# A recurrent kernel on one core: half A of the state chunk by chunk, and the x side of eight steps as seven block products

## The chip, the cores and the metric

The kernel runs on one core of a Trainium2 chip. The metric is the time of one execution on the device in microseconds; the kernel before takes 1693.7 us (median of three runs, 1693.68 to 1693.88). The engines are PE (matmul, with PEld for its weight loads), DVE (vector), ACT (scalar), POOL (GpSimd) and SP (which issues the DMAs).

## The reference, cut to what matters

A gated recurrence over 512 steps, for 8 sequences, with 512 inputs and 512 state units, all in float32. The output is x plus the states.

```python
def step(h, x_t):
    fused = sigmoid(concatenate([x_t, h], -1) @ w_W + w_b)
    hidden_state, output_state = split(fused, 2, -1)          # r and z
    memory_state = x_t @ wx_W + wx_b + hidden_state * (h @ wh_W + wh_b)
    h_new = output_state * h + (1.0 - output_state) * tanh(memory_state)
    return h_new, h_new
_, hs = lax.scan(step, h0, swapaxes(x, 0, 1))
return x + swapaxes(hs, 0, 1)
```

So every step needs three products of the state (for r, for z, and h @ wh_W), which wait for the step before, and three products of x, which wait for nothing and can be made for several steps at once.

## The kernel before, in words

**Layout.** State units are laid out in four chunks (`k` = 0 to 3) of 128 partitions. Chunks 0 and 1 are half A, chunks 2 and 3 half B (`hf` = 0, 1). A matmul takes 32 rows (8 sequences of a group of four steps, of which each step uses its own) as the stationary operand and writes 32 partitions of PSUM: the output units are cut into four column blocks (`j` = 0 to 3), each on its own 32 columns of the PE array, `mm(reg[32*j:32*j+32], lhsT, weights[k, j])`. Float32 makes two PE instructions of one matmul.

**The state's products.** Per step, 48 matmuls of 128 columns: banks R (r), G and H (halves of z and of h @ wh_W), each with four chunks and four blocks, in the order of line 27, `R0 R1 G0 G1 R2 R3 G2 G3 H0 H1 H2 H3`. Those with 0 and 1 need half A of the new state, those with 2 and 3 half B. The banks are doubled by groups of four steps, and PSUM accumulates onto what was copied there.

**The x side.** For a group of four steps, `prefill` (line 215) makes 16 matmuls of 384 columns (64 for half of z, 128 for r, 128 for the memory's x part, 64 for the other half of z: columns 64 to 448 of the bank `xp`) into one of two PSUM banks `xps[g % 2]`, in four rows of four blocks. `x_side` strings the groups together, and each step takes one row (line 276), behind the products of the state. `seed` (line 211) puts the biases into the bank before (a copy of 512 columns on ACT), `spread` (227) copies 128 columns each to R, G and H of the group (ACT), and `turn_x` (232) transposes X, the memory's part, to the tile `md1` (DVE).

**The step on DVE and ACT.** `turn_r` transposes r's products (tr) and puts their sigmoid into `md0`; `turn_h` transposes h @ wh_W to `md1`; `turn_z` transposes z's (tz) and puts sigmoid(-z) into `hd0`. `memory` makes r * hh + xx for pairs of slots as one running scan (multiply, add) into m, and its tanh into a slot of the state's tile `hT`; `update` makes the new state as a scan over three slots. They stand in the order tr A, tr B, then h, z, memory and update for half A, then the same for half B. In `scans` (line 280) half A is one scan of both chunks, half B two scans of one chunk; the tiles of half A are laid out rows first, those of half B chunks first (`pair`, line 134).

**Order.** It is written by hand (`manual_schedule`): each engine executes in the order in which the loop issues. At the end of a step stand: copies of the state (ACT), `turn_x` for the next group (DVE), one `spread` or, in the fourth step, `seed` (ACT), three small memsets (DVE), and the output sums x + h on POOL (`add`). The `tr` of half B waits for POOL's sums of seven steps before (line 312), as the tiles of the state go round in eight. SP's queue has the loads of x, three chunks of 16 steps ahead, and the stores of the output.

Of the kernel before, what the change touches and what calls it, by code (L numbers as in the profile page):

```python
# [28 lines left out]
FIRST = "Q0 x Q1 x Q2 x Q3 H0 H1 H2 H3"  # L29

BANKS = ("R", "G", "H")

XP = {"G": slice(0, 128), "R": slice(128, 256), "X": slice(256, 384), "H": slice(384, 512)}

# [2 lines left out]
def tile_cond_rnn_residual(  # L37
# [95 lines left out]

    def pair(n, name, rows, slots):

        if n == "A":
            return const.tile([P, rows, 2, slots], F32, name=name)
        return const.tile([P, 2, rows, slots], F32, name=name).rearrange("p c n s -> p n c s")


# [20 lines left out]
    for t_ in hd0[0] + hd0[1]:  # L161
        nc.gpsimd.memset(t_[:, :, :, 1], -1.0)
    idle = const.tile([P, IDLE], F32, name="idle")

    def state(hf, i, slot=2):

# [10 lines left out]
    def mm(out_, lhsT, rhs, start=False):  # L177
        nc.tensor.matmul(  # L178
            out_, lhsT, rhs, start=start, stop=False, skip_group_check=True
        )  # L180
# [30 lines left out]
    def seed(g):  # L211

        nc.scalar.copy(xps[g % 2], bias)

    def prefill(g):

        c, t0 = divmod(g * GS, TC)
        for k in range(NQ):
            for j in range(NQ):
                mm(  # L220
                    xps[g % 2][32 * j : 32 * j + 32, 64:448],
                    x_of(c, k, t0, GS),
                    wx[:, k, j, :],
                )
            yield

    def spread(g, names):

        for n in names:
            nc.scalar.copy(banks[g % 2][n], xps[g % 2][:, XP[n]])  # L230

    def turn_x(g, e):

        c0 = XP["X"].start + 32 * e
        nc.vector.transpose(
            md1[e // 2][g % 2][:, :, e % 2, 1], xps[g % 2][:, c0 : c0 + 32]
        )

    def take(it, n=None):
# [12 lines left out]
    later = x_side()  # L252
    spread(0, "RGH")
    for e in range(NQ):
        turn_x(0, e)

    pool_done = {}
    for i in range(T):
        g, s = divmod(i, GS)
        c, t = divmod(i, TC)  # L260
        ps = banks[g % 2]
        if t == 0 and c > 0:
            load_x(c + 3)
        if t == 0:
            ot = out_p.tile([P, TC, NQ, B], F32, tag="ot", name=f"ot_{c}")

        for n in (ORDER if i else FIRST).split():
            if n == "x":
                take(later, 1)
                continue  # L270
            bank, k = n[0], int(n[1])
            hs = hT[k // 2][i % NH][:, :, k % 2, 2]
            for j in range(NQ):
                to = xps[0][:, :256] if bank == "Q" else ps[bank]
                mm(to[32 * j : 32 * j + 32, :], hs, wh(bank, k, j))
        take(later, 1)

        rows = slice(B * s, B * s + B)

        def scans(hf, out_, d0, d1):  # L280

            for c_ in [slice(0, 2)] if hf == 0 else [slice(0, 1), slice(1, 2)]:
                nc.vector.tensor_tensor_scan(  # L283
                    *[t_[:, :, c_].rearrange("p n c s -> p (n c s)") for t_ in (out_, d0, d1)],
                    0.0,
                    ALU.mult,
                    ALU.add,
                )
# [12 lines left out]
        def turned(n, hf):  # L301
            t_ = work.tile([P, 2, 32], F32, tag=f"t{n}{hf}", name=f"t{n}{hf}_{i}")
            inst = nc.vector.transpose(t_.rearrange("p c n -> p (c n)"), raw[n][hf]).ins  # L303
# [15 lines left out]

        def turn_h(hf):  # L320
            nc.vector.transpose(  # L321
                md1[hf][g % 2][:, :, :, 0].rearrange("p n c -> p c n"), raw["h"][hf]
            )
# [12 lines left out]

        def memory(hf):

            m = work.tile([P, B, 2, 2] if hf == 0 else [P, 2, B, 2], F32, tag=f"m{hf}", name=f"m{hf}_{i}")
            if hf == 1:  # L340
                m = m.rearrange("p c n s -> p n c s")
# [25 lines left out]
        turn_h(1)  # L367
        turn_z(1)
        memory(1)
        update(1)  # L370
        for hf in range(2):
            act(("h", hf, (i + 1) % NH), state(hf, i + 1, 0), state(hf, i + 1), AF.Copy)
        if i < 3:
            load_x(i + 1)

        if g + 1 < NG:
# [105 lines left out]
```

## Time and profile before

| | us |
|---|---|
| median of three runs | 1693.7 |
| span of the profiled execution | 1691.7 |
| PE busy | 1680.3 (99%) |
| PE weight loads busy | 1467.6 (87%) |
| DVE busy | 1087.0 (64%) |
| ACT busy | 915.5 (54%) |
| POOL busy | 231.2 (14%) |
| matmuls of the x side, busy | 431.3, 4032 instructions, 486 ns each |

The profiled execution has no time of its own beside the span; the span is set against the median. Matmuls overlap each other (four column blocks, and one behind the other), so the busy time of a group counts more than its share of the step: what a group takes is read from the starts in the timeline. In the timeline a line merges neighbours of one kind; the bracket names the idle time before it and what ended it. PE ran at full granted clock (1.000) for the whole span. Nothing of note moves on the DMA queues after the start (17 GB/s).

### The profile page before, as it was taken

The page shows a single profiled execution, that of the slowest core. Times are in us where ns is not written, and L with a number is a line of the kernel's source. Part 1 is how long each engine was busy: PE and PEld are TensorE (multiplying, and loading weights), DVE is VectorE, ACT ScalarE, POOL GpSimd, SP SyncE. Part 2 cuts the span into 40 slices and gives each one's busy share as a digit, 9 for nine tenths or more (in the row PEclk, how much of TensorE's full clock was granted, in tenths as well). Part 3 has the DMA queues.
Part 4 walks back from the last instruction along what each step waited for, and adds up shares of the span by engine and source line. Part 5 has one row for each costly group of instructions (what it writes and reads, how often), then busy time and mean ns, then how long its engine had stood idle before and what let it go on. Part 6 is the DMA issues. An engine that isn't in the chain of part 4 may idle for free.

```text
span 1691.7 us, 121258 instructions
## 1 busy us (share of the span) xinstructions
PE 1680.3 (99%) x53230; PEld 1467.6 (87%) x53230; DVE 1087.0 (64%) x8229; ACT 915.5 (54%) x5121; POOL 231.2 (14%) x1032
## 2 busy tenths in 40 slices
PE   8999999999999999999999999999999999999998
PEld 6888888888888888888888888888888888888887
DVE  5666666666666666666666666666666666666666
ACT  3555555555555555555555555555555555555554
POOL 0111111111111111111111111111111111111111
PEclk9999999999999999999999999999999999999999
DMA  4000000000000000000000000000000000000000
GB/s 177 17 17 5 17 17 17 17 4 17 17 17 17 4 17 17 17 17 13 9 18 17 17 17 4 17 17 17 17 5 17 17 17 17 4 17 11 11 11 10
DMA packets 11483, 30.86 MB, mean 18 GB/s; under 512 B 1220, under 2 KB 1732, under 8 KB 10952
## 3 DMA queue, kind: packets, MB, share of 16 engines
q1 hardware_dynamic: 10800, 22.94, 3.9%
q8 instruction: 416, 6.82, 1.7%
q14 instruction: 115, 0.94, 0.2%
q10 hardware_dynamic: 152, 0.16, 0.0%
HBM read 14.70 MB, written 8.39 MB: 14 GB/s over the span
## 4 chain that ended last, share of the span: by engine, by line
PE 98%; DMA 1%; DVE 0%; ACT 0%; issue 0%; SPq 0%
PE R L178 26%; PE G L178 26%; PE H L178 26%; PE xp L178 19%; DMA whh<-in_whh_dram 1%; DMA head<-in_xh_dram 0%; DVE md1A L321 0%; DVE hTA L283 0%; ACT hd0A L205 0%; ACT hTA L205 0%; SPq L124 0%; DVE tz L303 0%; ACT hTB L205 0%; DVE hTB L283 0%; ACT hd0B L205 0%
## 5 line engine op out<-in xcount | busy, mean ns | idle before, releaser
L178 PE MATMUL xp<-wx,xin 128*32 128x384 f32 x4032 | 431.3, 486 | 0.0
L178 PEld LDWEIGHTS R<-wgr,hTA 128*32 128x32 f32 x8176 | 247.4, 135 | 206.8 <-DVE hTA L283 206.4
L303 DVE STREAM_TRANSPOSE tr<-R 128x64 f32<-128x64 f32 x1022 | 194.4, 229 | 309.1 <-PE R L178 309.1
L178 PE MATMUL R<-wgr,hTA 128*32 128x128 f32 x8176 | 330.9, 273 | 2.2 <-DVE hTA L283 2.2
L178 PE MATMUL H<-whh,hTA 128*32 128x128 f32 x8192 | 331.3, 273 | 0.8 <-DMA whh<-in_whh_dram 0.8
L178 PE MATMUL H<-whh,hTB 128*32 128x128 f32 x8192 | 331.2, 273 | 0.0
L178 PE MATMUL R<-wgr,hTB 128*32 128x128 f32 x8176 | 330.6, 273 | 0.0
L178 PE MATMUL G<-wgr,hTB 128*32 128x128 f32 x8176 | 330.6, 273 | 0.0
L178 PE MATMUL G<-wgr,hTA 128*32 128x128 f32 x8176 | 330.6, 273 | 0.0
L385 POOL TENSOR_TENSOR ot<-xin,hTB 128x16 f32<-128x16 f32 x503 | 126.4, 251 | 1415.6 <-DVE hTB L283 1324.0
L205 ACT ACTIVATE hd0B<-tz 128x16 f32<-128x16 f32 x512 | 114.9, 224 | 305.3 <-DVE tz L303 305.3
L205 ACT ACTIVATE md0A<-tr 128x16 f32<-128x16 f32 x512 | 119.6, 234 | 265.2 <-DVE tr L303 265.2
L178 PEld LDWEIGHTS H<-whh,hTA 128*32 128x32 f32 x8192 | 260.2, 136 | 1.2 <-DMA whh<-in_whh_dram 1.2
L178 PEld LDWEIGHTS G<-wgr,hTA 128*32 128x32 f32 x8176 | 259.8, 136 | 0.0
L178 PEld LDWEIGHTS H<-whh,hTB 128*32 128x32 f32 x8192 | 254.5, 122 | 0.0
L178 PEld LDWEIGHTS G<-wgr,hTB 128*32 128x32 f32 x8176 | 254.1, 122 | 0.0
L178 PEld LDWEIGHTS R<-wgr,hTB 128*32 128x32 f32 x8176 | 245.2, 122 | 0.0
L283 DVE TENSOR_TENSOR_SCAN hTA<-hd0A,hTA 128x48 f32<-128x48 f32 x512 | 132.1, 258 | 149.2 <-ACT hTA L205 149.2
L283 DVE TENSOR_TENSOR_SCAN hTB<-hd0B,hTB 128x24 f32<-128x24 f32 x1024 | 158.1, 196 | 104.0 <-ACT hTB L205 104.0
L205 ACT ACTIVATE hd0A<-tz 128x16 f32<-128x16 f32 x512 | 118.9, 232 | 111.4 <-DVE tz L303 111.4
L321 DVE STREAM_TRANSPOSE md1A<-G 128x64 f32<-128x64 f32 x511 | 156.8, 307 | 28.7
L205 ACT ACTIVATE hTB<-hTB 128x16 f32<-128x16 f32 x512 | 121.2, 237 | 81.1 <-DVE hTB L283 80.5
(62 smaller groups left out, 1680.2 us busy)
## 6 DMA issues: line engine op xcount, KB each, us to landing
xin<-in_x_dram SPq DMA_DIRECT2D x31, 256.0 KB, 3.8
out_dram<-ot SPq DMA_DIRECT2D x31, 256.0 KB, 3.3
wx<-in_wx_dram SPq DMA_DIRECT2D x4, 768.0 KB, 7.2
wgr<-in_wgr_dram SPq DMA_DIRECT2D x4, 512.0 KB, 9.7
whh<-in_whh_dram SPq DMA_DIRECT2D x1, 768.0 KB
whh<-in_wh_dram SPq DMA_DIRECT2D x1, 256.0 KB, 11.2
out_dram<-ot SPq DMA_DIRECT2D x1, 192.0 KB, 1.9
head<-in_xh_dram ACTq DMA_DIRECT2D x1, 144.0 KB, 5.2
```

The lines of the kernel that those rows point to most:

```text
L178: nc.tensor.matmul(out_, lhsT, rhs, start=start, stop=False, skip_group_check=True)
L205: inst = nc.scalar.activation(out_, in_, func, **kw).ins
L283: nc.vector.tensor_tensor_scan(*[t_[:, :, c_].rearrange("p n c s -> p (n c s)") for t_ in (out_, d0, d1)], 0.0, ALU.mult, ALU.add,)
L303: inst = nc.vector.transpose(t_.rearrange("p c n -> p (c n)"), raw[n][hf]).ins
L321: nc.vector.transpose(md1[hf][g % 2][:, :, :, 0].rearrange("p n c -> p c n"), raw["h"][hf])
L385: return engine.tensor_tensor(ot[:, t, 2 * hf : 2 * hf + 2, :].rearrange("p c n -> p n c"), x_of(c, slice(2 * hf, 2 * hf + 2), t, 1).rearr ...
```

## The change

1. **Half A chunk by chunk.** `scans` makes two scans of one chunk for half A as for half B, each followed by its own tanh, and the tiles of half A get half B's layout. R's second quarter (R1) then waits for the second chunk by itself.

2. **The x side of eight steps as seven block products.** Eight steps are two groups of 32 rows, the inputs two halves (`kh`), the outputs two halves of 192 columns (`ch`). The product of 2x2 blocks by 2x2 blocks has eight block products; a scheme of the Strassen kind makes it with seven, on sums of x blocks (`x_sum`, on POOL, per eight steps, tiles `sx`) and of weight blocks (`weight_sum`, on POOL, once, tiles `tw`). The sums over products accumulate in four PSUM areas of 192 columns (AL and BE in bank `xp0`, GA and DE in `xp1`); what several results share is copied from one area to another in between (ACT), and one part (`both`) is added on POOL to the last two quarters, in SBUF (`even`, `odd`). `turn_x` and the copy of H read there; R and G are still copied from PSUM. Each block product is 8 matmuls of 192 columns, so eight steps take 56, and a step takes seven, `take(later, 7)`. The biases come as copies of 192 columns.

3. **The start.** Groups 1 to 3 are still made in the old way, in the steps up to 4 (two rows a step from step 1 on); octets from the third on come from the new products, beginning in step 5.

```diff
+HALF = 192
+AL, BE = (0, slice(64, 256)), (0, slice(256, 448))
+GA, DE = (1, slice(64, 256)), (1, slice(256, 448))
     def pair(n, name, rows, slots):
-        if n == "A":
-            return const.tile([P, rows, 2, slots], F32, name=name)
         return const.tile([P, 2, rows, slots], F32, name=name).rearrange("p c n s -> p n c s")
+    def late(g):
+        if g == 0:
+            return xps[0][:, 256:512]
+        return even if g % 2 == 0 else odd[g // 2 % 2]
     def spread(g, names):
         for n in names:
-            nc.scalar.copy(banks[g % 2][n], xps[g % 2][:, XP[n]])
+            src = late(g)[:, 128:256] if n == "H" else xps[g % 2][:, XP[n]]
+            nc.scalar.copy(banks[g % 2][n], src)
+    def weight_sum(n):
+        a, b = [
+            (wx_of(0, 1), wx_of(0, 0)),
+            (wx_of(1, 1), tw[0]),
+            (wx_of(1, 1), wx_of(0, 1)),
+            (wx_of(1, 0), tw[1]),
+        ][n]
+        nc.gpsimd.tensor_tensor(tw[n], a, b, ALU.subtract)
+    def x_sum(o, n):
+        t_ = [q[o % 2] for q in sx]
+        a, b, op = [
+            (x_half(o, 1, 0), x_half(o, 1, 1), ALU.add),
+            (t_[0], x_half(o, 0, 0), ALU.subtract),
+            (x_half(o, 0, 0), x_half(o, 1, 0), ALU.subtract),
+            (x_half(o, 0, 1), t_[1], ALU.subtract),
+        ][n]
+        nc.gpsimd.tensor_tensor(t_[n], a, b, op)
+    def products(o):
+        t_ = [q[o % 2] for q in sx]
+        for to, lhs, rhs in (
+            (AL, x_half(o, 0, 0), wx_of(0, 0)),
+            (DE, t_[0], tw[0]),
+            (BE, t_[1], tw[1]),
+            (AL, x_half(o, 0, 1), wx_of(1, 0)),
+            (GA, t_[2], tw[2]),
+            (BE, t_[3], wx_of(1, 1)),
+            (GA, x_half(o, 1, 1), tw[3]),
+        ):
+            for k in range(2):
+                for j in range(NQ):
+                    mm(reg(to)[32 * j : 32 * j + 32], lhs[:, k], rhs[:, k, j])
+                    yield
     def x_side():
-        for g in range(1, NG):
-            yield from prefill(g)
+        for o in range(2, NG // 2):
+            yield from products(o)
+    first = {g: prefill(g) for g in (1, 2, 3)}
-        take(later, 1)
+        if i < 5:
+            take(first[(i + 3) // 2], 2)
+        else:
+            take(later, 7)
-            for c_ in [slice(0, 2)] if hf == 0 else [slice(0, 1), slice(1, 2)]:
+            for c_ in (slice(0, 1), slice(1, 2)):
-            if s < 3:
-                spread(g + 1, "RGH"[s])
-            elif g + 3 < NG:
-                seed(g + 3)
+        if u == 0:
+            spread(2 * o + 1, "G")
+            if o and nxt:
+                nc.scalar.copy(reg(GA), reg(BE))
+        elif u == 1:
+            spread(2 * o + 1, "H")
+        elif u == 2 and nxt:
+            last = odd[(o + 1) % 2][:, :HALF]
+            nc.scalar.copy(last, reg(GA))
+            nc.gpsimd.tensor_tensor(last, last, both, ALU.add)
+        elif u == 3 and nxt:
+            if o:
+                nc.scalar.copy(even[:, :HALF], reg(BE))
+                nc.gpsimd.tensor_tensor(even[:, :HALF], even[:, :HALF], both, ALU.add)
+            spread(2 * o + 2, "R")
+        elif u == 4 and nxt:
+            spread(2 * o + 2, "G")
+            nc.scalar.copy(reg(AL), bias[:, AL[1]])
+            x_sum(o + 2, 0)
+        elif u == 5 and nxt:
+            spread(2 * o + 2, "H")
+            nc.scalar.copy(reg(DE), step_bias)
+            x_sum(o + 2, 1)
+        elif u == 6 and two:
+            nc.scalar.copy(reg(BE), reg(AL))
+            x_sum(o + 2, 2)
+        elif u == 7 and nxt:
+            spread(2 * o + 3, "R")
+            nc.scalar.copy(both, reg(DE))
+            x_sum(o + 2, 3)
+        if i < 4:
+            weight_sum(i)
```

Here `o, u` are the octet and the step in it, `nxt` and `two` say that there are one and two more octets; special cases of the first octet are cut.

More of the change, by code (lines that the diff above doesn't have):

```diff
@@ L163, in tile_cond_rnn_residual @@
     idle = const.tile([P, IDLE], F32, name="idle")
+    tw = [const.tile([P, 2, NQ, HALF], F32, name=f"tw{n}") for n in range(4)]
+    sx = [[const.tile([P, 2, GS * B], F32, name=f"sx{n}{q}") for q in range(2)] for n in range(4)]
+    step_bias = const.tile([P, HALF], F32, name="stepbias")
+    even = const.tile([P, 256], F32, name="even")
+    odd = [const.tile([P, 256], F32, name=f"odd{q}") for q in range(2)]
+    both = const.tile([P, HALF], F32, name="both")
     def state(hf, i, slot=2):
@@ L225, in prefill, with reg, wx_of, x_half @@
             yield
+    def late(g):
+        if g == 0:
+            return xps[0][:, 256:512]
+        return even if g % 2 == 0 else odd[g // 2 % 2]
     def spread(g, names):
         for n in names:
-            nc.scalar.copy(banks[g % 2][n], xps[g % 2][:, XP[n]])
+            src = late(g)[:, 128:256] if n == "H" else xps[g % 2][:, XP[n]]
+            nc.scalar.copy(banks[g % 2][n], src)
     def turn_x(g, e):
-        c0 = XP["X"].start + 32 * e
         nc.vector.transpose(
-            md1[e // 2][g % 2][:, :, e % 2, 1], xps[g % 2][:, c0 : c0 + 32]
+            md1[e // 2][g % 2][:, :, e % 2, 1], late(g)[:, 32 * e : 32 * e + 32]
         )
+    def reg(r):
+        return xps[r[0]][:, r[1]]
+    def wx_of(kh, ch):
+        return wx[:, 2 * kh : 2 * kh + 2, :, HALF * ch : HALF * ch + HALF]
+    def x_half(o, n, kh):
+        return x_of(o // 2, slice(2 * kh, 2 * kh + 2), 8 * (o % 2) + GS * n, GS)
+    def weight_sum(n):
[30 more added lines that the diff above has]
+                    yield
     def take(it, n=None):
@@ L268, in tile_cond_rnn_residual @@
             if n == "x":
-                take(later, 1)
+                take(first[1], 1)
                 continue
@@ L275, in tile_cond_rnn_residual @@
                 mm(to[32 * j : 32 * j + 32, :], hs, wh(bank, k, j))
-        take(later, 1)
+        if i < 5:
+            take(first[(i + 3) // 2], 2)
+        else:
+            take(later, 7)
         rows = slice(B * s, B * s + B)
         def scans(hf, out_, d0, d1):
-            for c_ in [slice(0, 2)] if hf == 0 else [slice(0, 1), slice(1, 2)]:
+            for c_ in (slice(0, 1), slice(1, 2)):
                 nc.vector.tensor_tensor_scan(
@@ L337, in memory @@
         def memory(hf):
-            m = work.tile([P, B, 2, 2] if hf == 0 else [P, 2, B, 2], F32, tag=f"m{hf}", name=f"m{hf}_{i}")
-            if hf == 1:
-                m = m.rearrange("p c n s -> p n c s")
+            m = work.tile([P, 2, B, 2], F32, tag=f"m{hf}", name=f"m{hf}_{i}").rearrange("p c n s -> p n c s")
             for c_ in scans(hf, m, md0[hf][g % 2][:, rows], md1[hf][g % 2][:, rows]):
@@ L374, in tile_cond_rnn_residual @@
             load_x(i + 1)
+        o, u = divmod(i, 2 * GS)
+        nxt, two = o + 1 < NG // 2, o + 2 < NG // 2
+        if i == 0:
+            nc.scalar.copy(odd[0], xps[1][:, 256:512])
         if g + 1 < NG:
             turn_x(g + 1, s)
-            if s < 3:
-                spread(g + 1, "RGH"[s])
-            elif g + 3 < NG:
-                seed(g + 3)
+        if i == 0:
+            spread(1, "R")
+        if u == 0:
[4 more added lines that the diff above has]
+            spread(2 * o + 1, "H")
+        elif u == 2 and o == 0:
+            seed(3)
+            nc.scalar.copy(even, xps[0][:, 256:512])
+        elif u == 2 and nxt:
[8 more added lines that the diff above has]
+        elif u == 4 and nxt:
+            if o == 0:
+                nc.scalar.copy(odd[1], xps[1][:, 256:512])
+            spread(2 * o + 2, "G")
+            if two:
+                nc.scalar.copy(reg(AL), bias[:, AL[1]])
+                x_sum(o + 2, 0)
+        elif u == 5 and nxt:
+            spread(2 * o + 2, "H")
+            if two:
+                nc.scalar.copy(reg(DE), step_bias)
[5 more added lines that the diff above has]
+            spread(2 * o + 3, "R")
+            if two:
+                nc.scalar.copy(both, reg(DE))
+                x_sum(o + 2, 3)
+        if i < 4:
+            weight_sum(i)
+        if i == 4:
+            nc.gpsimd.tensor_tensor(step_bias, bias[:, BE[1]], bias[:, AL[1]], ALU.subtract)
         for n in range(IDLE):
```

## The prediction

> **What bounds the kernel now.** I read the page's busy shares and chain first, then the timeline of one steady step, then the timeline of the last steps, in which no x work is left, and then the groups.
>
> ```profile
> PE 1680.3 (99%) x53230; PEld 1467.6 (87%) x53230; DVE 1087.0 (64%) x8229; ACT 915.5 (54%) x5121; POOL 231.2 (14%) x1032
> PE 98%; DMA 1%; DVE 0%; ACT 0%; issue 0%; SPq 0%
> ```
>
> PE is always busy and the chain of waits lies on it, but matmuls are pipelined, so that alone does not say how much shorter a step may get. The timeline says it:
>
> ```profile
> 802.17 0.31 DVE L321 STREAM_TRANSPOSE md1A<-G 128x64 f32<-128x64 f32 x1
> ...
> 802.52 0.23 DVE L283 TENSOR_TENSOR_SCAN m<-md0A,md1A 128x32 f32<-128x32 f32 x1
> ...
> 802.78 0.22 ACT L205 ACTIVATE hTA<-m 128x16 f32<-128x16 f32 x1
> 802.78 0.86 PE L178 MATMUL xp<-wx,xin 128*32 128x384 f32 x8
> 803.04 0.26 DVE L283 TENSOR_TENSOR_SCAN hTA<-hd0A,hTA 128x48 f32<-128x48 f32 x1 [0.29 <-ACT hTA L205]
> 803.21 0.23 DVE L321 STREAM_TRANSPOSE md1B<-H 128x64 f32<-128x64 f32 x1
> 803.35 0.48 PEld L178 LDWEIGHTS R<-wgr,hTA 128*32 128x32 f32 x16 [0.41 <-DVE hTA L283]
> ...
> 803.43 0.65 PE L178 MATMUL R<-wgr,hTA 128*32 128x128 f32 x16
> ...
> 803.95 0.31 DVE L283 TENSOR_TENSOR_SCAN hTB<-hd0B,hTB 128x24 f32<-128x24 f32 x2 [0.20 <-ACT hTB L205]
> ...
> 804.43 0.26 ACT L230 COPY R<-xp 128x128 f32<-128x128 f32 x1
> ...
> 805.29 0.23 ACT L205 ACTIVATE md0A<-tr 128x16 f32<-128x16 f32 x1 [0.59 <-DVE tr L303]
> ```
>
> The first x row of step 1 begins at 22.44 us and that of step 504 at 1664.74: 3.265 us a step, without jitter. In it the x row (8 instructions; every matmul is two) takes 0.64 to 0.65, and the 96 instructions of R, G and H the other 2.62. A column block of 32 gets a quarter of them: 24 rounds of 128 columns are 109 ns each, two rounds of 384 are 322 ns each, so a round of 192 is 162.5 ns by the straight line between them. The weight load for R starts 0.08 before its matmul.
>
> The last steps show the step without x work, so the time of the recurrence alone:
>
> ```profile
> 1668.56 0.67 PE L178 MATMUL R<-wgr,hTA 128*32 128x128 f32 x16 [0.34 <-DVE hTA L283]
> ...
> 1669.43 0.42 PEld L178 LDWEIGHTS R<-wgr,hTB 128*32 128x32 f32 x16
> 1669.49 0.62 PE L178 MATMUL R<-wgr,hTB 128*32 128x128 f32 x16
> ...
> 1671.78 0.45 PE L178 MATMUL R<-wgr,hTA 128*32 128x128 f32 x8 [0.36 <-DVE hTA L283]
> ```
>
> From R to R it is 3.22 (the next ones follow at 1675.00, 1678.24 and 1681.46: 3.225 in the mean). So PE is ahead of the recurrence by only 0.04 us a step. Two loops close there. **Loop A**: R, G done, md1A, m, tanh, hTA, load of R; PE waits 0.36 for it. A load that is not ahead costs 0.05 (R to G is 0.49 there against 0.44). **Loop B**: the same on to md1B and hTB, then the load of the second half of R, which starts 0.06 ahead of its matmul where others are 0.10 or 0.11 ahead. It needs 0.05 of that, so loop B is 3.21 to 3.22 too.
>
> ```profile
> L178 PE MATMUL xp<-wx,xin 128*32 128x384 f32 x4032 | 431.3, 486 | 0.0
> L321 DVE STREAM_TRANSPOSE md1A<-G 128x64 f32<-128x64 f32 x511 | 156.8, 307 | 28.7
> L283 DVE TENSOR_TENSOR_SCAN m<-md0B,md1B 128x16 f32<-128x16 f32 x1024 | 133.0, 172 | 0.0
> L283 DVE TENSOR_TENSOR_SCAN m<-md0A,md1A 128x32 f32<-128x32 f32 x512 | 115.0, 225 | 0.0
> L321 DVE STREAM_TRANSPOSE md1B<-H 128x64 f32<-128x64 f32 x512 | 115.7, 226 | 0.4 <-PE H L178 0.4
> ```
>
> Half B shows here what half A will cost: chunk by chunk, and with its layout.
>
> **The x side on PE.** Eight steps take 56 matmuls of 192 columns instead of 32 of 384: 10,752 columns for 12,288, an eighth less. By the mean that is 0.645 to 0.57 a step. But a step gets seven matmuls, and seven do not divide by four blocks: three blocks get two (4 rounds of 162.5 = 0.650), one gets one (0.325). As the order goes on round the blocks, each block is the short one in one step of four. The next step's R needs the state, and the state needs R and G of all blocks, so a short block gains only down to the recurrence. Beginning level, the slowest block takes 2.62 + 0.65 = 3.27 in three steps, and in the fourth, its own short one, the recurrence's time L: a step is (3 x 3.27 + L) / 4. The same short step has let the others catch up before.
>
> **Half A by chunks.** First chunk of m 172 ns for 225, its tanh 198 for 225: the hTA scan starts 0.08 sooner. It is about 0.20 for 0.26, so R's load moves from 803.35 to about 803.22: loop A is 0.13 shorter. R's second quarter now waits by itself for the second chunk, about 0.12 after the first; the first quarter covers 0.22. For loop B: a pair of scans holds DVE 0.23 (803.95 to the next instruction at 804.18), the single one 0.17 (803.04 to 803.21), so md1B starts 0.08 - 0.06 = 0.02 sooner. The new layout makes md1A more like md1B, 307 to 226 ns; some 0.04 of the difference is rather that it follows a wait (tr: 0.25 for the first, 0.21 for the second), and tz and hd0A hold m's tanh at nearly the old place. Bounds for loop B: 0 and 0.10 shorter; I take 0.035, near the row of the pair, so L = 3.18. Two more scans a step add (2 x 172 - 225) + (2 x 196 - 258) = 253 ns on DVE, in its waits of 0.29 for tanh.
>
> **ACT.** Per eight steps the two copies of 512 columns (591 ns) go, up to seven of 192 come, between 265 (the 128-column row) and 591; by the line 0.32. A step has at most a 128 and a 192 copy. Ahead of md0A stand 0.59 idle after one copy (805.29): even 591 fits just. If not, md0A of the next step is late, and with it m. Copies that wait for x products come 0.9 us or more after these.
>
> **POOL.** Two sums of 192 columns and four of 64 per eight steps, ahead of the output sums in its queue. A sum of 16 columns is 0.25; a memset goes from 120 ns (16) to 297 (192), 1.0 ns a column. So 192 columns are 0.43 by that, 3.0 in proportion; the value is needed some 2.6 us later (the X transpose of 804.18, a step on, against a copy that ends near 804.8), with 0.6 idle behind that transpose. Output sums come later; the tr that waits for POOL waits for those of seven steps ago. The four weight sums of 1536 columns, once, are 1.8 us by the memset's slope, 24 in proportion; the first is needed in step 6 and the last in step 11, some 40 us later. I take the slope (nearest in size): nothing. In proportion PE would stall 50 us once.
>
> **Start and end.** Groups 2 and 3 now go two rows a step in steps 1 to 4: 4 x 0.645 = +2.6. Then 496 steps with seven products (5 to 500), and eleven without x instead of seven. SP and the DMAs stay as they are; DVE's transposes of X read copies made a step or more before.
>
> **Sum** against the profiled span, 1691.7 (the median of the runs is 1693.7, so 2.0 lie around it): a step (9.81 + 3.18) / 4 = 3.2475, so 496 x -0.0175 = -8.7; +2.6; four steps without x -0.3; seven last ones -0.3. Together -6.7: **1687.0**. With L from 3.12 to 3.22 a step is 3.2325 to 3.2575, and the time 1679 to 1692.
>
> [...] The x row has eight instructions in 0.645 us at 486 ns each. If a matmul's two instructions stand side by side in the queue, four blocks could not do that with starts in queue order: the second matmul would start behind the first's second half, 0.32 later, and the row would take 1.6. So blocks run ahead of each other, as my sum needs. [...]
>
> **Rivals.**
> 1. *The blocks stay level* (slower). Place: the first R matmul after the x row. Every step 2.62 + 0.65 = 3.27, 496 x 0.005 = +2.5, with +2.6 and -0.6: 1698. For it: every block of one step starts within 0.05 of the others now. It decides from the point where the short block may not start over 0.03 ahead. Chance 0.12.
> 2. *New waits in the tail of the step* (slower): two ACT copies or POOL's sums beside DVE hold md0A or md1A. 0.05 us in half of 496 steps is +12.4 on the forecast: 1699. For it: ACT has 0.59 left, and its PSUM to SBUF copies and POOL beside scans are not in the trace. Chance 0.14.
> 3. *Loop B is not shortened*: L = 3.22, 1692, or a little over with a small stall: no change. Chance 0.18.
> 4. *Full eighth*: blocks average out, 2.62 + 0.57 = 3.19 a step, 496 x -0.075 = -37, 1658. Against it: L would have to be 2.95. Chance 0.02.
>
> The forecast (1679 to 1691) has 0.54. A measurement of this kernel tells 0.2%, 3.4 us, from no change: faster is under 1690.3, slower over 1697.1. Faster 0.57, same 0.18, slower 0.25. The range goes from the low end with a little for a shorter loop, 1677, to the two slow rivals, 1700.
>
> **What would show it.** Right: steps in fours, three of 3.27 and one of about 3.18, in the starts of R; loads of R for hTA some 0.2 ahead in the long steps; the last eleven steps about 3.18 apart. Wrong: all steps 3.27 (rival 1); steps over 3.27 at fixed places of the eight, with md0A or md1A late (rival 2); all near 3.19 (rival 4).

## The result and the profile after

| | before | after |
|---|---|---|
| median, us | 1693.79 (1693.68 to 1693.95) | 1700.31 (1699.86 to 1701.04) |
| span of the profiled execution | 1691.7 | 1698.1 |
| PE busy, matmuls | 1680.3, 53,230 | 1682.4, 56,206 |
| POOL busy | 231.2 | 384.0 |

The change costs 0.39% (ratio 1.0039, 95% interval 1.0027 to 1.0051). It was predicted at 1687.0, faster, with a range to 1700. Against the forecast span of 1691.7 - 6.7 = 1685.0 the profiled execution is 13.1 us long.

Busy shares and the chain, from the page of the kernel after:

```profile
PE 1682.4 (99%) x56206; PEld 1623.5 (96%) x56206; DVE 1127.2 (66%) x9253; ACT 974.5 (57%) x5946; POOL 384.0 (23%) x1409
PE 97%; DVE 1%; DMA 1%; ACT 0%; issue 0%
L188 PE MATMUL xp<-tw,sx 128*32 128x192 f32 x2976 | 221.1, 326 | 0.0
```

PE is as busy as before, over more instructions; nothing here says what went wrong. What tells is the length of each step, from one start of `md1A<-G` on DVE to the next (there is one a step). Medians over steps 13 to 492, by the step `u` of the octet in which the interval begins:

| kernel | u = 5, 6, 7 | u = 0 | u = 1, 2, 3 | u = 4 | steps 1 to 4 |
|---|---|---|---|---|---|
| before | 3.265 | 3.265 | 3.265 | 3.265 | 3.265 |
| after | 3.270 | 3.164 | 3.270 | **3.317** | **5.51, 5.55, 5.55**, 3.91 |

The forecast fours are there: three steps of 3.270 and a short one of 3.16, and the blocks do run ahead of one another. In the timeline of the kernel after, around the end of an x row:

```profile
842.26 0.51 PE L188 MATMUL xp<-tw,sx 128*32 128x192 f32 x8
842.58 0.33 PE L188 MATMUL xp<-wx,sx 128*32 128x192 f32 x2
842.60 0.33 PE L188 MATMUL xp<-tw,sx 128*32 128x192 f32 x1
842.68 0.31 PE L188 MATMUL R<-wgr,hTA 128*32 128x128 f32 x1
842.75 0.33 PE L188 MATMUL xp<-wx,sx 128*32 128x192 f32 x2
842.76 0.33 PE L188 MATMUL xp<-tw,sx 128*32 128x192 f32 x1
842.83 0.59 PE L188 MATMUL R<-wgr,hTA 128*32 128x128 f32 x12
```

R of the next step starts at 842.68, before the last x matmuls of the step (842.75, 842.76), though it stands behind them in the program. The last steps, without x work, follow each other at the recurrence's own time, 3.16:

```profile
1680.21 0.25 DVE L389 STREAM_TRANSPOSE md1A<-G 128x64 f32<-128x64 f32 x1
1683.37 0.25 DVE L389 STREAM_TRANSPOSE md1A<-G 128x64 f32<-128x64 f32 x1
1686.53 0.25 DVE L389 STREAM_TRANSPOSE md1A<-G 128x64 f32<-128x64 f32 x1
```

What was not forecast stands in two places. One is the start: in steps 1 to 3, POOL makes three of the four weight sums, and VectorE's m scan of half A beside them takes ten times its time. VectorE and POOL in the timeline of the kernel after:

```profile
26.55 3.47 POOL L273 TENSOR_TENSOR tw<-wx 128x1536 f32<-128x1536 f32 x1
27.19 0.25 DVE L389 STREAM_TRANSPOSE md1A<-G 128x64 f32<-128x64 f32 x1
27.36 0.21 DVE L371 STREAM_TRANSPOSE tz<-G 128x64 f32<-128x64 f32 x1
27.50 2.66 DVE L351 TENSOR_TENSOR_SCAN m<-md0A,md1A 128x16 f32<-128x16 f32 x2
30.35 0.31 DVE L351 TENSOR_TENSOR_SCAN hTA<-hd0A,hTA 128x24 f32<-128x24 f32 x2 [0.19 <-ACT hTA L215]
```

The sum ends at 30.02 and the pair of scans, 0.26 elsewhere, at 30.16; the two transposes under the same sum have their usual 0.25 and 0.21. The other place is the second short step of each octet, u = 4:

```profile
847.49 0.59 POOL L466 TENSOR_TENSOR even<-even,both 128x192 f32<-128x192 f32 x1 [2.27 <-ACT even L465]
848.04 0.25 POOL L495 TENSOR_TENSOR ot<-xin,hTB 128x16 f32<-128x16 f32 x1
848.25 0.25 POOL L495 TENSOR_TENSOR ot<-xin,hTA 128x16 f32<-128x16 f32 x1
848.45 0.32 POOL L284 TENSOR_TENSOR sx<-xin 128x64 f32<-128x64 f32 x1
848.48 0.42 DVE L351 TENSOR_TENSOR_SCAN m<-md0A,md1A 128x16 f32<-128x16 f32 x2
```

`even` waits for its copy; the output sums and `sx`, behind it in POOL's queue, come 1.0 later than in other steps, and `sx` starts 0.03 ahead of the m scan, which takes 0.42 for 0.26. In a step of 3.27, 0.11 of such a delay (3.27 - 3.16) would be hidden behind PE; in the short step it is loop A that sets the time, so all of it counts.

The 13.1 us are then: the start 5.507 + 5.546 + 5.554 + 3.910 - 4 x 3.910 = +4.9; u = 4, 62 x (3.317 - 3.18) = +8.5; the other short steps, 62 x (3.162 - 3.18) = -1.1; the eleven last ones -0.3; and four odd long steps (3.4 to 3.7) with +1.0, of which more below. Together 13.0.

### The profile page after: what moved, and what is told of

Its sections match the earlier page's. It is cut to its first block, busy times and chain, and to the rows that moved or that the text cites. A ratio compares the mean times of both kernels' runs of the same rounds, so it can differ in the third digit from the quotient of the medians.

```text
span 1698.1 us, 129801 instructions
## 1 busy us (share of the span) xinstructions
PE 1682.4 (99%) x56206; PEld 1623.5 (96%) x56206; DVE 1127.2 (66%) x9253; ACT 974.5 (57%) x5946; POOL 384.0 (23%) x1409
## 4 chain that ended last, share of the span: by engine, by line
PE 97%; DVE 1%; DMA 1%; ACT 0%; issue 0%
PE R L188 29%; PE H L188 26%; PE G L188 25%; PE xp L188 18%; DMA whh<-in_whh_dram 1%; DVE m L351 0%; DMA rows<-in_bias_dram 0%; DVE md1A L389 0%; DVE hTA L351 0%; ACT hd0A L215 0%; DVE tz L371 0%; ACT hTA L215 0%; DVE rows L120 0%; ACT hTB L215 0%; DVE hTB L351 0%
## 5 line engine op out<-in xcount | busy, mean ns | idle before, releaser
L188 PE MATMUL R<-wgr,hTA 128*32 128x128 f32 x8176 | 409.5, 277 | 6.1 <-DVE hTA L351 6.1
L188 PE MATMUL G<-wgr,hTA 128*32 128x128 f32 x8176 | 380.4, 273 | 0.0
L188 PE MATMUL R<-wgr,hTB 128*32 128x128 f32 x8176 | 368.7, 276 | 0.0
L188 PE MATMUL H<-whh,hTA 128*32 128x128 f32 x8192 | 349.6, 273 | 1.0 <-DMA whh<-in_whh_dram 0.8
L188 PE MATMUL G<-wgr,hTB 128*32 128x128 f32 x8176 | 348.8, 273 | 0.0
L188 PEld LDWEIGHTS R<-wgr,hTA 128*32 128x32 f32 x8176 | 275.6, 123 | 30.5 <-DVE hTA L351 22.4
L188 PEld LDWEIGHTS G<-wgr,hTA 128*32 128x32 f32 x8176 | 279.3, 122 | 0.0
L351 DVE TENSOR_TENSOR_SCAN hTA<-hd0A,hTA 128x24 f32<-128x24 f32 x1024 | 157.7, 195 | 103.2 <-ACT hTA L215 103.1
L188 PE MATMUL xp<-tw,sx 128*32 128x192 f32 x2976 | 221.1, 326 | 0.0
L188 PE MATMUL xp<-wx,xin 128*32 128x192 f32 (+1 forms) x2048 | 165.6, 331 | 0.0
```

Of the source, the lines that this page charges most:

```text
L188: nc.tensor.matmul(out_, lhsT, rhs, start=start, stop=False, skip_group_check=True)
L351: nc.vector.tensor_tensor_scan(*[t_[:, :, c_].rearrange("p n c s -> p (n c s)") for t_ in (out_, d0, d1)], 0.0, ALU.mult, ALU.add,)
```

## The experiments

**The theories.** T1: a POOL sum of two SBUF operands holds a VectorE scan of two SBUF operands until it ends. Its rivals are that the scans are late for another reason, or that taking the holds away brings nothing because another wait follows.

**First: take POOL's sums away from the scans.** `x_late` issues `sx` behind the output sums of the step; `tw_early` makes the weight sums on VectorE, three before step 0 and the fourth in quarters at the ends of steps 1 to 4; `both_moved` does both; `a_only` is the kernel before with half A by chunks and the old x side.

```diff
x_late:
-                x_sum(o + 2, 0)                  # and 1, 2, 3 in their places
+        if u >= 4 and two:                       # behind the two output sums
+            x_sum(o + 2, u - 4)
tw_early:
-        nc.gpsimd.tensor_tensor(tw[n], a, b, ALU.subtract)
+        nc.vector.tensor_tensor(tw[n][:, :, js], a[:, :, js], b[:, :, js], ALU.subtract)
-        if i < 4:
-            weight_sum(i)
+        if 1 <= i <= 4:
+            weight_sum(3, slice(i - 1, i))
a_only:
-            for c_ in [slice(0, 2)] if hf == 0 else [slice(0, 1), slice(1, 2)]:
+            for c_ in (slice(0, 1), slice(1, 2)):
```

> The four sums of x blocks of an octet move behind the output sums of their steps on POOL's queue; nothing else changes. Theory (POOL's sums hold up VectorE's scans, which read two operands from SBUF): in the octet's step 4 the m scan of half A no longer meets POOL, that step goes from 3.317 back to 3.16 us, 62 x 0.155 = 9.6 us less, 1690.7 us. Rival (the long step comes from the two ScalarE copies at the end of step 3 making the sigmoids late): they are untouched, the time stays at 1700.

> The four weight sums go from POOL to VectorE: three before the first step, where VectorE is idle, the fourth in quarters at the ends of steps 1 to 4. Theory (each weight sum on POOL, 3.47 us, holds the m scan until it ends): steps 1 to 3 go from 5.54 us to the 3.91 of their two x rows, 4.9 us less, 1695.4 us. Rival (these steps are long through their two rows of x matmuls and what follows from them): 1700, steps 1 to 3 as long as before.

> Both moves together. Theory: the savings add, 9.6 + 4.9 = 14.5 us less than the changed kernel, 1685.8 us, 8 us under the kernel before. Steps then go in fours, three of 3.27 and one of 3.16. Rival (as in the two single moves): 1700.

> The kernel before with half A chunk by chunk and the layout of half B, and the old x side. Theory (PE's stream sets the step, half A only shortens the recurrence under it): steps stay at 3.265, only the seven last steps without x go from 3.225 to 3.155, 0.5 us less, 1693.3. Rival (two more scans a step on VectorE cost on the path): steps over 3.265, some us slower.

Measured: `a_only` 1692.98 (ratio 0.9995, 0.9986 to 1.0003), no change, with all steps at 3.265 and the last ones at 3.16: half A by chunks does its part, which the x side hides. None of the others came to its forecast: `x_late` 1704.75 (1.0057, 1.0044 to 1.007) and `tw_early` 1705.3 (1.0068, 1.0054 to 1.0082) are slower than the kernel after at the median, and `both_moved`, 1697.74 (1.0029, 1.0017 to 1.004), is 2.6 below it at the median but goes from 1693.4 to 1705.6 in eleven runs.

Place by place T1 holds. With the weight sums gone, steps 1 to 4 are 3.91 each, as forecast; with `sx` later, the m scan of u = 4 is back at 0.26. The same place as above in `x_late`, VectorE and POOL:

```profile
849.09 0.60 POOL L466 TENSOR_TENSOR even<-even,both 128x192 f32<-128x192 f32 x1 [2.26 <-ACT even L465]
849.64 0.25 POOL L491 TENSOR_TENSOR ot<-xin,hTB 128x16 f32<-128x16 f32 x1
849.84 0.25 POOL L491 TENSOR_TENSOR ot<-xin,hTA 128x16 f32<-128x16 f32 x1
850.07 0.26 DVE L351 TENSOR_TENSOR_SCAN m<-md0A,md1A 128x16 f32<-128x16 f32 x2
```

This step takes 3.16, as forecast, with ScalarE's copies at the end of the step before untouched; so the copies, the rival in the expectation, are not what held it. But new long steps come, 3.34 to 4.0 us, irregular, in bands: 59, 45 and 56 of the 480 steps, where the kernel before and `a_only` have none and the kernel after has four. In `both_moved`, steps 13 to 492 take 16.1 us more than the pattern of three 3.27 and one 3.16. PE in one of these, timeline of `both_moved`:

```profile
1386.43 0.39 PE L188 MATMUL H<-whh,hTA 128*32 128x128 f32 x4
1387.03 0.49 PE L188 MATMUL H<-whh,hTA 128*32 128x128 f32 x9 [0.21 <-issue]
1387.29 0.28 PE L188 MATMUL H<-whh,hTB 128*32 128x128 f32 x3
```

In the middle of a row whose operands have long been there, PE stops, and the profile shows nothing that it waits for ("issue"). That is a second effect, with theories of its own.

**Second: the hold by itself.** On the kernel before, where POOL is free, one POOL instruction is added to each step, on tiles that nobody reads (one run each). `lock_two` releases a sum of 64 columns by md1A's transpose; `lock_late` a sum of 192 columns by the second tr; `lock_memset`, at the same place, writes 512 columns of zeros, so that POOL is as long at it but reads nothing.

```diff
lock_late (lock_memset: nc.gpsimd.memset(waste[0], 0.0)):
         turn_r(1)
+        if i:
+            tc.add_manual_dep(nc.gpsimd.tensor_tensor(waste[0], waste[1], waste[2], ALU.add).ins, turned_r.name, SYNC)
         turn_h(0)
```

> The kernel before with one more POOL sum in each step, of two SBUF tiles of 64 columns into a third that nobody reads, released by the transpose of h of half A, so that it lies beside the m scan of half A. T1 (a POOL sum of two SBUF operands holds a VectorE scan of two SBUF operands until it ends): the scan m<-md0A takes 0.40 to 0.55 us instead of 0.26, half A's loop grows from 3.225 to 3.36 to 3.5 and takes over the step: 1740 to 1815. Rival (POOL's sums were late or queued, and hold nothing): scan 0.26, time 1693 to 1696.

> The kernel before with one more POOL sum in each step, of two SBUF tiles of 192 columns into a third that nobody reads, released by the second transpose of r, so that it runs from about 844.7 to 845.3 in the profile's step and meets the m scan of half A (from 844.95). In the first such kernel the sum began when the scan had already ended. T1 (a POOL sum of two SBUF operands holds a VectorE scan of two SBUF operands until it ends): the scan m<-md0A takes 0.45 to 0.65 us instead of 0.23 and half A's loop grows by as much: step 3.45 to 3.65, time 1785 to 1890. Rival (no hold): scan 0.23 to 0.26, 1693 to 1697. The transposes from PSUM beside it (md1A, tz) keep 0.30 and 0.21 in both.

> As the run with the 192-column sum, but POOL writes 512 columns of zeros and reads nothing. T1 in the form that two operands read from SBUF hold the scan: scan 0.23 to 0.26, 1693 to 1696. If any POOL access to SBUF holds it: scan 0.4 or more and a longer step, 1740 to 1850.

`lock_two`, 1693.5, missed its mark: the sum runs from 845.06, when the m scan (844.95 to 845.18) is already under way, and both have their usual time. It does not decide on T1. `lock_late` met it, 1773.37. Its timeline:

```profile
846.22 0.32 DVE L327 STREAM_TRANSPOSE md1A<-G 128x64 f32<-128x64 f32 x1
846.31 0.60 POOL L360 TENSOR_TENSOR waste<-waste,waste 128x192 f32<-128x192 f32 x1 [0.69 <-DVE tr L307]
846.40 0.21 DVE L307 STREAM_TRANSPOSE tz<-G 128x64 f32<-128x64 f32 x1
846.57 0.42 DVE L287 TENSOR_TENSOR_SCAN m<-md0A,md1A 128x32 f32<-128x32 f32 x1
```

The scan takes 0.42 for 0.23 and ends 0.08 behind the sum (846.91). The step grows from 3.265 to 3.421: loop A at 3.225 and 0.19 more is 3.415. The range given, 1785 to 1890, was too high, as the scan is held by 0.19 and not by 0.22 to 0.42. `lock_memset` is 1693.43: the memset, 0.53 long from 847.85, covers the whole scan at 848.13, which keeps its time. The groups of `lock_late` and of `lock_memset`:

```profile
L287 DVE TENSOR_TENSOR_SCAN m<-md0A,md1A 128x32 f32<-128x32 f32 x512 | 213.8, 418 | 0.0
```

```profile
L287 DVE TENSOR_TENSOR_SCAN m<-md0A,md1A 128x32 f32<-128x32 f32 x512 | 115.0, 225 | 0.0
```

So in these runs it is not POOL at work, nor its writing, but its reading of SBUF that holds the scan: beside the sum the scan takes 0.42, beside the memset 0.23. Transposes that read PSUM go on under the sum: md1A's takes 0.32 and tz 0.21 in `lock_late`, 0.31 and 0.21 in `lock_memset`. In `lock_two`, where the sum starts with 0.12 of the scan to go, it takes 0.32, as `sx` of the same 64 columns does in the kernel after.

**Third: the long steps.** T3: TensorE's instructions come too late. T4: the uneven column blocks, or the lost wait for hTA, do it, whatever the number of instructions. Every matmul is two load and two matmul instructions (8192 of each on `H<-whh,hTA`, for 8 matmuls in each of 512 steps), so a step of 48 + 7 matmuls has 220 instructions in 3.24 us, where the kernel before has 208 in 3.265. How they arrive is in the pages of before and after, in the busy shares and the DMA queues:

```profile
PE 1680.3 (99%) x53230; PEld 1467.6 (87%) x53230; DVE 1087.0 (64%) x8229; ACT 915.5 (54%) x5121; POOL 231.2 (14%) x1032
...
q8 instruction: 416, 6.82, 1.7%
```

```profile
q8 instruction: 439, 7.19, 1.8%
```

106,460 instructions (loads and matmuls) are 416 times 256 to within one block; 112,412 are 439 times 256. In `split` (448 transfers for 114,652) and `wide` (412 for 105,468) it comes out too. So, by these four counts, this queue brings PE's instructions, 256 to a transfer, one every 4.01 us before, every 3.75 in the kernel after and every 3.78 in `both_moved` (medians).

`split` is the kernel before with each x matmul of 384 columns cut into two of 192: more instructions, level blocks, nothing else. `wide` is `both_moved` with half as many x matmuls, of twice the width; it leaves out the distinction of the half-width operands, so it computes something else and serves for its time alone. `merged` joins the matmuls of R and G for chunks 0 and 1 into one of 256 columns, `merged_a` does it on `a_only` as a control.

```diff
split:
-                mm(xps[g % 2][32 * j : 32 * j + 32, 64:448], x_of(c, k, t0, GS), wx[:, k, j, :])
+                for e in range(2):
+                    mm(xps[g % 2][32 * j : 32 * j + 32, 64 + 192 * e : 256 + 192 * e],
+                       x_of(c, k, t0, GS), wx[:, k, j, 192 * e : 192 * e + 192])
wide:
-            for k in range(2):
-                for j in range(NQ):
-                    mm(reg(to)[32 * j : 32 * j + 32], lhs[:, k], rhs[:, k, j])
+            for j in range(NQ):
+                mm(xps[to[0]][32 * j : 32 * j + 32, 64:448], lhs[:, 0], wx[:, 0, j])
-            take(later, 7)
+            take(later, 2 if i % 4 == 0 else 4)
merged, merged_a:
-ORDER = "R0 R1 G0 G1 R2 R3 G2 G3 H0 H1 H2 H3"
+ORDER = "Q0 Q1 R2 R3 G2 G3 H0 H1 H2 H3"
```

> The kernel before with each x matmul of 384 columns split into two of 192: 56 instead of 52 matmuls a step, 224 instead of 208 instructions of TensorE in a step of 3.27 us, nothing else changed, and the blocks stay level. T3: irregular long steps appear as in the kernels of the first call, 1696.5 to 1712. T4: none; four rounds of 325 us-thousandths become eight of 162.5, with at most 0.005 us a step for the split: 1693.8 to 1696.4.

> The kernel with both of POOL's sums moved out of the way, and the x side as half as many matmuls of twice the width: each product is one matmul of 384 columns per column block instead of two of 192 (28 in eight steps instead of 56), issued 4, 4, 4 and 2 to a step. TensorE's columns per step are the same, its instructions fall from 220 to 206 a step. What it computes from x is not the reference's: the half-width operands are not told apart, and each product takes one of its two chunks of rows. T3 (late supply of TensorE's instructions): no irregular long steps, excess over 3.27 us below 2, time 1684 to 1688; three steps of 3.27 and one of 3.16. T4 (the lost wait for hTA or the uneven blocks, whatever the number of instructions): excess of 8 to 14 us as in the kernel with both moved, 1694 to 1700.

> The kernel with both of POOL's sums moved out of the way, and in the recurrent part the matmuls of R and G for the chunks 0 and 1 joined into one of 256 columns each (R and G then share a bank of PSUM): 47 instead of 55 matmuls a step, the same columns, so 188 instead of 220 instructions of TensorE in a step. T3 (the long steps come from a late supply of TensorE's instructions): the long steps go, the excess over 3.27 us falls from some 14 us to below 2, and the time is 1697.7 - 14 + 2 = about 1685.8 (1683 to 1688). T4 (the long steps come from the column blocks that run ahead of one another, or from the lost wait for hTA, whatever the number of instructions): the excess stays, 1695 to 1700. Both could be covered by a cost of the shared bank, which merged_a shows.

> The kernel before with half A by chunks and the same joining of R and G in chunks 0 and 1: 44 instead of 52 matmuls a step. It is the control for the shared bank. T3 and T4 both: steps stay at 3.265 us and the time at 1693.0 (1692 to 1694.5). If the shared bank or the later R of chunk 1 has a price, it is the excess over that.

`split` is 1703.52 (1.0059, 1.0045 to 1.0072), with 33 steps over 3.34 us: more instructions alone bring the long steps, with level blocks. PE's wait for hTA goes as well there (6 of 512 steps keep it), so this run does not part the two. `wide` is 1689.26 (0.9973, 0.9962 to 0.9984) with no step over 3.266. It is 1.3 over its range because only one step of eight is short there (3.163; presumably because its rows of 4, 4, 4 and 2 begin at another block each time), for which 1693.8 + 2.6 (start) - 62 x 0.10 - 0.9 (the last steps at 3.16) is 1689.3.

`merged` (1847.21) and `merged_a` (1845.3) say nothing on T3. R and G share a tile there, in one bank of PSUM, and tr waits for the last matmul of that tile, G's, instead of R's. Waits in `merged_a`:

```profile
DVE tr L302 <- PE GR L176: 500.7, 511, 1.1
ACT md0A L204 <- DVE tr L302: 454.5, 512, 4.9
PEld GR L176 <- DVE hTA L282: 346.5, 510, 0.9
```

Loop A gets the 0.3 us a step (3.562), which the control shows to be the price of the sharing alone; the expectation had missed it. Whether it is the bank or the common tile that sets this wait, no run tells.

The gaps fit T3 in two more ways. In `split`, 10 of the 11 gaps of over 0.2 us between the starts of two matmuls end 1.0 to 1.35 us ahead of the start of an instruction transfer, in `both_moved` 23 of 30. With a transfer every 3.75 us, that stretch would hold one in ten by chance. And they stand at one place of the blocks. Counted in order of start, with PE's loads, matmuls and own semaphore instructions, from the first one recorded, the instruction behind such a gap in steps 13 to 492 is preceded by 193 or 194 instructions over a multiple of 256: all 30 gaps of `both_moved`, all 11 of `split`, all 25 of `x_late` and all 23 of `tw_early`, whatever the bank or the row. In `both_moved`, the 16 places from 184 to 199 together take 13.6 us more than 16 average ones, of 16.1 us lost; in the kernel before the difference is 0.0. So PE stops at a fixed place of its blocks of 256: what stops it goes with the blocks, not with a place in the step.

**Fourth: rate or lead, and the blocks.** `x_only` is `both_moved` with the old half A; `level` issues 8, 8, 8 and 4 x matmuls instead of 7 each; `split_half` splits the x matmuls of every second step only. `mix2` takes seven products in every second octet only and the 32 old matmuls of 384 columns in the others, `mix3` the old way in every third; `mix2_level` and `mix3_level` are these with 8, 8, 8 and 4. T3a: each stretch has the loss of its own rate; T3b: PE's sequencer gets ahead in the quieter steps and lives on it.

```diff
mix2 (mix3: o % 3 != 0), on both_moved:
+    def seven(o):
+        return o % 2 == 0
     def products(o):
+        if not seven(o):
+            for n in range(2):
+                for k in range(NQ):
+                    for j in range(NQ):
+                        mm(xps[n][32 * j : 32 * j + 32, 64:448], x_half(o, n, k // 2)[:, k % 2], wx[:, k, j, :])
+                        yield
+            return
...
-            take(later, 7)
+            take(later, 7 if seven((i - 5) // 8 + 2) else 4)
level:
-            take(later, 7)
+            take(later, 4 if i % 4 == 0 else 8)
```

> The kernel with both of POOL's sums moved, and half A of the recurrent part as in the kernel before: the x side alone. The short step of four is then set by half A's old loop of 3.225: (3 x 3.27 + 3.225)/4 = 3.259, 496 steps at -0.006 from 3.265 and a start 2.6 longer: 1693.9 without late instructions. T3: 220 instructions in 3.259 us, so irregular long steps remain, with excess of 5 to 15 us: 1699 to 1709. T4 (the lost wait for hTA): the short step has a wait again, the excess falls below 3: 1694 to 1697.

> The kernel with both of POOL's sums moved, and its 28 x matmuls of four steps issued 8, 8, 8 and 4 instead of 7 each, so that all column blocks are level in every step. 220 instructions a step on the mean (224 in three of four). T3: irregular long steps as before, 1694 to 1706. T4 (uneven blocks are the cause): none, 1684 to 1688.

> The kernel before with half of its x matmuls split into two of 192 columns: 208 and 224 instructions in alternate steps, 216 on the mean, in 3.265 to 3.27 us. T3a: a part of the 8.5 us excess of the kernel with all split, 3 to 6: 1697 to 1701. T3b: the steps of 208 give the lead back: excess below 1, 1693.8 to 1696.

> The kernel with both of POOL's sums moved, and seven products in every second octet only; the others take 32 matmuls of 384 columns as the kernel before does (208 instructions a step at 3.265 us). Without late instructions 31 octets give 0.18 us each up again: 1685 + 31 x 0.18 = 1690.7. If the supply of instructions counts step by step (T3a), the octets of seven keep their long steps and the excess is about half of 13.8: 1695 to 1699. If TensorE's sequencer gets a lead in the other octets and lives on it (T3b): excess below 3, 1690 to 1693.5.

> The same with every third octet plain: without late instructions 1685 + 21 x 0.18 = 1688.8. T3a: two thirds of the excess, 1696 to 1700. T3b: the lead must last for two octets, excess below 4: 1688.5 to 1693.

> The kernel with seven products in every second octet, and these issued 8, 8, 8 and 4 matmuls to four steps. T3b (a lead of TensorE's instructions won in the plain octets, 208 a step, and in level blocks): the kernel with 7 a step had 31 octets of seven at 0.18 us each gained and 1.6 us of long steps left; these go: 1689.5 to 1691. If uneven blocks had no part: 1691.1 as with 7 a step.

> The same with every third octet plain. Without late instructions 1688.8. T3b with a part of the uneven blocks: long steps fall from 3.7 us to below 2, 1688.8 to 1690.8. If the unevenness had no part: 1691.5 as with 7 a step.

All kernels but the `lock` and `merged` ones, by PE instructions per step. "Waits" counts the steps in which the load of R waits for hTA, of 512; "long" the steps over 3.34 us of steps 13 to 492. Both are from the one profiled execution; the times are medians of several, and the profiled one can lie at an end of their range (`mix3` 1694.6 of 1689.2 to 1694.6, `mix2_level` 1691.1 of 1691.1 to 1692.3).

| kernel | instructions a step | waits | long | time, us (ratio, interval) |
|---|---|---|---|---|
| before | 208 | 510 | 0 | 1693.8 |
| `a_only` | 208 | 510 | 0 | 1692.98 (0.9995, 0.9986 to 1.0003) |
| `wide` (other x side) | 206 | 506 | 0 | 1689.26 (0.9973, 0.9962 to 0.9984) |
| `mix2` | 208 and 220 by octets | 256 | 6 | 1691.08 (0.9984, 0.9975 to 0.9993) |
| `mix2_level` | the same | 318 | 2 | 1691.81 (0.9988, 0.9979 to 0.9997) |
| `mix3` | 208, 220, 220 by octets | 179 | 13 | 1691.51 (0.9986, 0.9977 to 0.9994) |
| `mix3_level` | the same | 260 | 9 | 1691.94 (0.9992, 0.9984 to 1.0001) |
| `split_half` | 208 and 224 by steps | 258 | 4 | 1697.28 (1.0021, 1.0011 to 1.003) |
| after | 220 | 69 | 4 | 1700.31 (1.0039, 1.0027 to 1.0051) |
| `level` | 220 | 131 | 31 | 1691.29 (0.9984, 0.9974 to 0.9995) |
| `x_only` | 220 | 24 | 32 | 1701.13, one run |
| `tw_early` | 220 | 38 | 45 | 1705.3 (1.0068, 1.0054 to 1.0082) |
| `both_moved` | 220 | 10 | 56 | 1697.74 (1.0029, 1.0017 to 1.004) |
| `x_late` | 220 | 13 | 59 | 1704.75 (1.0057, 1.0044 to 1.007) |
| `split` | 224 | 6 | 33 | 1703.52 (1.0059, 1.0045 to 1.0072) |

The wait column, as the waits of before and of `both_moved` show it (us in total, times, longest):

```profile
PEld R L178 <- DVE hTA L283: 206.4, 510, 0.6
```

```profile
PEld R L188 <- DVE hTA L354: 4.8, 10, 0.5
PEld xp L188 <- issue: 6.3, 26, 0.6
PEld H L188 <- issue: 4.2, 14, 0.8
```

T3 holds throughout: no long steps at 206 to 208 (the longest of 480 is 3.266 in the kernel before), few where a half or a third of the steps or octets have 208, 31 to 59 where all have 220 or more, but for the kernel after. Within T3 the counts speak for the lead (T3b): T3a would have left `mix2` half of the 56 and `split_half` half of 33, and they have 6 and 4. The time of `split_half`, 1697.28, does lie in T3a's range and over T3b's; but its long steps cost 1.6 us by the trace, nearer to T3b's "below 1" than to T3a's 3 to 6, and the rest of the 3.9 us by which its span is longer than before are 1.2 in the split steps, 3.270 each, and 1.1 ahead of step 13. Uneven blocks fall as the cause by `split` and `level`, whose blocks are level; but they have a part: `level` loses 8.7 us over the pattern where `both_moved` loses 16.1, and its time lies between the two forecasts. The lost wait for hTA goes with the long steps in nearly all rows, so these runs don't part it from the number of instructions; it is the fixed place in the blocks of 256 (193 or 194 over a multiple) that ties the stalls to the supply, and by T3b the wait is where PE gets ahead. In the mixed kernels the level issue brought nothing that can be told (1691.81 for 1691.08). `x_only` was as T3 expected.

Other DMA traffic seems to have a part too: of the 294 long steps in the table, 49 are the second of a chunk of 16, where 18 would be by chance, and nearly all bytes of the other queues move in the first, with the loads of x. No run tests it.

So there are versions below both kernels that compute the same: `mix2`, `mix2_level`, `mix3` and `level` have their intervals under 1. `mix2` has the lowest median and is among the steadiest of them (1690.4 to 1692.0; `level` goes from 1686.5 to 1695.4): 0.16% under before (0.07 to 0.25) and 9 us under after. By what a measurement of this kernel can tell from no change, 0.2%, that is little.

**What stays open.** Why the kernel after has four long steps only: with the hold at the start alone (`x_late`) there are 59, with the hold in u = 4 alone (`tw_early`) 45, with both almost none. From step 13 on, `tw_early` runs the same instructions as the kernel after, with the same medians (3.318 and 3.317 in u = 4), so the slack of these steps by itself does not explain it; the cause stays open. What PE's sequencer does in a gap cannot be seen in the profile.

## Why the prediction was wrong

- **What bounds the kernel, and the loops**: right. Step 3.265 by PE, loops A and B just under it.
- **The x side on PE**: right. Seven matmuls on four blocks make three steps of 3.270 (forecast 3.27) and a short one. Matmuls of different column blocks do not start in the order of the program here (R at 842.68 before x at 842.75), and so rival 1 fell.
- **L**: 3.18 forecast, 3.156 to 3.164 measured: half A by chunks brought loop A what was expected, and loop B some 0.06 instead of 0.035. A gain of 1.4 us on the forecast.
- **ACT**: right, two copies a step fit.
- **POOL: the step that failed.** "The first is needed in step 6 ... nothing" asked only whether the sums come in time for their readers. They do. That they keep VectorE from its scans was put at nothing in the sum, although each sum was priced and its place in POOL's queue given. The prices were low too, 3.47 for 1.8 us and 0.60 for 0.43, inside the bounds given. The hold costs 4.9 us at the start and 8.5 in u = 4, which is the whole miss; the shorter L and the odd long steps nearly cancel. Rival 2 named "POOL's sums beside DVE" and came out at 1699, but with 0.05 us in half of the steps as a guess: it was 0.155 in one step of eight and 1.6 in three steps, so its time is near by luck. The trace of before could not have told: there POOL's sums (0.25 us, at 801.07 and 801.28) lie where VectorE has memsets or waits.
- **Start**: +2.6 by two x rows a step is right without the hold (3.91 in `tw_early`).
- **Missing from the sum**: the supply of PE's instructions. The change adds 12 instructions to a step of which it takes 0.02 us, and the sum had only columns in it. In the kernel after, it cost about 1 us; without the holds it costs 16 (the profiled execution of `both_moved`), so the gain of 6.7 was not to be had by putting POOL right alone.

## What to carry to other kernels

Before work goes to an "idle" POOL, see what VectorE does at that time: here a POOL sum that reads SBUF stopped a VectorE scan with two SBUF operands until it ended (0.42 us for 0.23 in `lock_late`), while transposes from PSUM went on beside it (0.32 and 0.21), and a POOL memset did not stop the scan (0.23). Work saved on PE in columns but paid in more instructions was not free here, where PE is the bound (16.1 us lost in `both_moved`, at 220 instructions a step for 208): count the instructions per step as well, and see whether PE still has a wait (510 steps of 512 before, 10 in `both_moved`). And measure a step's length by its place in the cycle, since the means of all groups looked as forecast here while one step in eight carried the loss.

## What was not expected of the hardware

- The hold lasted until about the end of the POOL sum: 2.66 us for 0.26 under a POOL sum of 3.47 (kernel after), 0.42 for 0.23 under one of 0.60 (`lock_late`), and 0.23 under a memset of 0.53 (`lock_memset`).
- POOL's sums took 0.25 us for 16 columns, 0.32 for 64, 0.60 for 192 and 3.47 for 1536.
- PE stalls of 0.2 to 0.8 us at one place of its blocks of 256 instructions (193 or 194 over a multiple of 256) appeared at 220 instructions in 3.24 us (14.7 ns each; 31 to 59 long steps of 480, but 4 in the kernel after) and not at 208 in 3.265 (15.7 ns; none), and with half of the steps or octets at 208 there were 4 (`split_half`) and 6 (`mix2`).
